# Cross attention of a perceiver layer: dividing the products instead of the probabilities, with the inverses sent round through DRAM

## The chip, the cores and the metric

The kernel runs on one core of a Trainium2 chip. The core has engines that work side by side, each through its own queue of instructions in a fixed order: TensorE (PE in the profile; loads of its stationary operand are PEld), VectorE (DVE), ScalarE (ACT) and GpSimd (POOL), and SyncE (SP), which here only issues transfers. They meet through semaphores. The metric is the device time of one execution in microseconds. Three runs of the kernel before took 698.24, 698.39 and 699.4 us; the median is 698.39.

## The reference, cut to what matters

The input is `x` (32 batches of 64 latents, 128 wide), a context (32 batches of 1601 tokens, 128 wide) and a mask of the context's tokens. The layer is a cross attention, a self attention and a feed-forward part, each added to `x`; only the first concerns the change.

```python
xn = layernorm(x, ln_x_g, ln_x_b)              # here x is the context
ln = layernorm(latents, ln_l_g, ln_l_b)        # latents are the normalised x
q = ln @ Wq
kv = jnp.concatenate((xn, ln), axis=1) @ Wkv
k, v = jnp.split(kv, 2, axis=-1)
q, k, v = (heads(q) * scale, heads(k), heads(v))   # 16 heads of 64
sim = jnp.einsum('bhid,bhjd->bhij', q, k)
sim = jnp.where(mask_full[:, None, None, :], sim, max_neg)
attn = jax.nn.softmax(sim.astype(jnp.float32), axis=-1).astype(sim.dtype)
out = jnp.einsum('bhij,bhjd->bhid', attn, v)
out = out.transpose(0, 2, 1, 3).reshape(b, m, INNER) @ Wout
return layernorm(out, ln_o_g, ln_o_b)
...
x = x + _L0_xattn_ref(ctx_1024, _layernorm(x, axis=-1), mask_BxS2_bk0, ...)
x = x + _L0_attn_ref(_layernorm(x, axis=-1), ...)
x = x + _L0_ffn_ref(_layernorm(x, axis=-1), ...)
```

The mask is true for the tokens that are used, and in this input those are at most the last 400 of a batch, beside the 64 latents, which are always keys too. The kernel sorts the batches by need and gives each 64 to 448 rows of context, so its rows are short.

## The kernel before, in words

**Weights.** For each head the kernel multiplies query and key weights into one 128 x 128 matrix (`a_sb`), and value and output weights into another (`b_sb`). So keys and values are never built: logits are products of the queries `qT` with the normalised tokens `xT`, the probabilities are multiplied with the same tokens (`xn`), and `b_sb` turns the result into the output.

**Tiles.** The 32 batches are sorted by the number of tokens that they need and paired, one long (u = 0) with one short (u = 1), into 16 tiles `t`. `CAPS` gives the rows: 512 logits beside 128 in the first eight tiles, 512 beside 256 in one, 384 beside 256 in six, 384 beside 384 in the last. At run time the kernel chooses among three arms by the mask; this input takes the narrow one, in which a step does both batches.

**Steps.** A step is one pair of heads `c` (0 to 7) of one tile, 128 steps in all. On its 128 partitions lie 2 heads x 64 latents. `logits` (line 522) does, for each u: a matmul into a PSUM bank `bank_s` (line 537, there are two such banks), one VectorE instruction that adds the mask's addends, writes the sums to `s` and finds the extreme `low` (line 540), and one ScalarE instruction that takes the exponential in place and sums the rows into `den` (line 545). Then VectorE takes the reciprocal of `den` (line 551), and multiplies each `s` with it (line 554).

`turned` transposes the probabilities on TensorE, two steps later (lines 573 and 583, copied to `pT` by ScalarE at 576 and 584). `attend` (line 590) runs after odd steps, three steps later for u = 0 and four for u = 1: it multiplies `xn` with the probabilities of two pairs of heads, for 256 columns in a bank `bank_m` (line 601), and VectorE copies the bank to `oT` (line 606). In `oT` the 128 partitions are the width of a token, not heads and latents. `project` (line 632) multiplies with `b_sb`, and adds and normalises.

**What runs in between.** Work of other tiles is laid beside the steps by `at(step, ...)`: the queries of the next tile (line 513), the normalising of its context (`prepare`: VectorE, GpSimd for a power at line 438, ScalarE at line 471), its transposes, the loads of the tile after it, and the self attention of the tile before (lines 654 to 778). The softmax of the self attention uses a bank `bank_s` too, which VectorE empties at line 719; line 774 adds the self attention's output to `x`.

**Order.** The lists made by `at` give the order of the program's text. The framework's scheduler then lays the instructions of each engine into one fixed order when the program is built, so that instructions can stand a little earlier or later than in the text. Within an engine's queue nothing overtakes. SP's queue holds the transfers of the loop: the context of tile t + 2 (lines 414 and 417, in up to two pieces), its mask (line 424) and `x` (line 403). The first piece waits until TensorE is done with the buffer's former tokens (there are three buffers).

**After the loop** come the feed-forward part and the stores (lines 885 to 988), with nothing of the cross attention.

Of the kernel before, what the change touches and what calls it, by code (L numbers as in the profile page):

```python
# [8 lines left out]
FP = mybir.dt.float32  # L9
# [3 lines left out]
ALU = mybir.AluOpType  # L13
# [3 lines left out]
P = 128  # L17
D = 128
B = 32
SL = 64  # L20
# [16 lines left out]
def perceiver_layer(  # L37
# [8 lines left out]
    nc = tc.nc  # L46
# [5 lines left out]
    early = ExitStack()  # L52
    look = early.enter_context(tc.tile_pool(name="look", bufs=1, side="right"))
    small = ctx.enter_context(tc.tile_pool(name="small", bufs=4))
    ps_s = ctx.enter_context(tc.tile_pool(name="ps_s", bufs=2, space=PSUM))
    ps_t = ctx.enter_context(tc.tile_pool(name="ps_t", bufs=3, space=PSUM))
    ps_m = ctx.enter_context(tc.tile_pool(name="ps_m", bufs=3, space=PSUM))
# [4 lines left out]
    def bank_m():  # L62
        return ps_m.tile([P, 512], FP, tag="m", name="bank_m")

    def bank_s():
        return ps_s.tile([P, 512], FP, tag="s", name="bank_s")


    def piece(eng, shape, src, name, pool=prep, dtype=FP):
        r = pool.tile(shape, dtype, name=name, tag=name)  # L70
        eng.dma_start(out=r, in_=src)
        return r
# [45 lines left out]
    for cap in sorted(set(CAPS), reverse=True):  # L118
# [7 lines left out]
        out=back, in0=mk, in1=back, scale=1.0, scalar=0.0,  # L126
# [10 lines left out]
    for r in range(0, B, 8):  # L137
        nc.vector.max(out=rank[:, r : r + 8], in_=left)
        if r + 8 < B:
            nc.vector.match_replace(  # L140
                out=left, in_to_replace=rank[:, r : r + 8], in_values=left, imm_value=-1.0
# [152 lines left out]
    for k, clip in enumerate((clip_x, clip_down)):  # L294
        c = piece(nc.scalar, [P, 1], clip.partition_broadcast(P), f"clip{k}", const)
# [55 lines left out]
    def attention(actx, name, caps):  # L351
# [6 lines left out]
        two = actx.enter_context(tc.tile_pool(name=f"two{name}", bufs=2))  # L358
        narrow = max(caps) <= SW
# [4 lines left out]
        def shape(t, u):  # L364

            nt, rest = divmod(cap(t, u) - SL, P)
            return nt, rest, [P] * (1 + nt) + [rest] * (rest > 0), SL + cap(t, u)
# [29 lines left out]
            for i in range(2):  # L397
                nc.gpsimd.memset(vxs[i], 0.0)

        masks, lns, lnTs, xTs, qTs, oTs, probs, pTs = {}, {}, {}, {}, {}, {}, {}, {}  # L400

        def load_x(t, u):
            nc.sync.dma_start(
# [117 lines left out]

        def logits(t, c, us):

            den = small.tile([P, len(us)], FP, tag=f"den{name}", name="den")
            for i, u in enumerate(us):
                sk = shape(t, u)[3]
                w = qTs[t][:, u, 2 * c : 2 * c + 2, :].rearrange("p h i -> p (h i)")
                s = two.tile(
                    [P, k_max[u]], FP, tag=f"s{u}" if narrow else "s", name=f"s{t}_{u}_{c}",
                    bufs=4 if narrow else 2,  # L530
                )[:, :sk]

                pieces = [(k, min(k + 512, sk)) for k in range(0, sk, 512)]
                low = small.tile([P, len(pieces)], FP, tag=f"low{name}{u}", name="low")
                for j, (k, e) in enumerate(pieces):
                    ps = bank_s()
                    nc.tensor.matmul(  # L537
                        ps[:, : e - k], lhsT=w, rhs=xTs[t, u][:, k:e], start=True, stop=True
                    )
                    nc.vector.tensor_tensor_reduce(  # L540
                        out=s[:, k:e], in0=ps[:, : e - k], in1=addends[u][t % NA][:, k:e],
                        scale=-1.0, scalar=3e38 if j == 0 else low[:, j - 1 : j],
                        op0=ALU.add, op1=ALU.min, accum_out=low[:, j : j + 1],
                    )
                nc.scalar.activation(  # L545
                    s, s, AF.Exp, bias=low[:, len(pieces) - 1 :], scale=-1.0,
                    accum_out=den[:, i : i + 1],
                )
                probs[t, u, c] = s
            rden = small.tile([P, len(us)], FP, tag=f"rden{name}", name="rden")  # L550
            nc.vector.reciprocal(rden, den)  # L551
            for i, u in enumerate(us):
                s = probs[t, u, c]
                nc.vector.tensor_scalar_mul(s, s, rden[:, i : i + 1])  # L554

        def turned(t, c, u):

# [32 lines left out]
        def attend(t, c, u):  # L590

            if t not in oTs:
                oTs[t] = two.tile(
                    [P, H, 2, SL], FP, tag="oT", name=f"oT{t}", bufs=2 if narrow else 1
                )
            pT = pTs.pop((t, u, c))
            po = bank_m()
            xn = xns[u][t % NX]
            tiles = shape(t, u)[2]
            for n, k in enumerate(tiles):  # L600
                nc.tensor.matmul(  # L601
                    po[:, : 2 * P], lhsT=xn[:k, n, :],
                    rhs=pT[:k, n].rearrange("p o c -> p (o c)"),
                    start=(n == 0), stop=(n == len(tiles) - 1),
                )
            nc.vector.tensor_copy(  # L606
                oTs[t][:, 2 * c : 2 * c + 4, u, :],
                po[:, : 2 * P].rearrange("p (h i) -> p h i", i=SL),
            )

        def moments(src, twice=False):
# [182 lines left out]
        for i, (t, c, us) in enumerate(steps):  # L794
            for u in us:
                at(i + 2, turned, t, c, u)
                if c % 2:
                    at(i + 3 + (u if narrow else 0), attend, t, c - 1, u)
# [71 lines left out]
        for i in range(max(later) + 1):  # L870
            if i < len(steps):
                logits(*steps[i])
            for f, args in later.get(i, ()):
                f(*args)
# [5 lines left out]
    for k in tc.Switch(which, 3):  # L880
        with ExitStack() as actx:
            attention(actx, "abc"[k], (CAPS, [SW] * B, [S2] * B)[k])


    with ExitStack() as fctx:
# [41 lines left out]
        for i in range(NB):  # L927
# [8 lines left out]
            for c, w in enumerate(widths):  # L936
# [6 lines left out]
                h = hT[i][:w, c, :]  # L943
# [89 lines left out]
```

## Time and profile before

| | |
|---|---|
| median of three runs | 698.39 us |
| the profiled execution: its own time | 700.29 us |
| the profiled execution: span, first to last instruction | 698.6 us |
| granted clock of TensorE, mean | 0.962 |
| busy: TensorE, VectorE, ScalarE, GpSimd | 622.9, 522.9, 409.2, 129.1 us |
| line 554, multiplying the probabilities | 256 instructions, 89.1 us |
| line 551, reciprocals | 128 instructions, 20.5 us |
| line 606, emptying the bank of `attend` | 128 instructions, 53.3 us |
| transfers of the execution | 12.00 MB, 17 GB/s over the span |

The page of the profile tells of one execution. Busy time is the sum of the instructions' durations on an engine; neighbours can overlap at their ends, and the end of a matmul is modelled, so a distance between two starts tells more than a duration. A line of a group reads: line of the kernel, engine, operation, output and inputs with shapes, count | busy us, mean ns of one | idle us of the engine just ahead of these instructions, and what ended it. A wait reads: who, for whom, us in total, how often, the longest. A line of a timeline reads: start, duration, instruction, count, and in brackets the idle time before it.

### The profile page before, as it was taken

Reading aid. Unit: us, or ns where it says so; the run is one execution under the profiler, and the core shown is the slowest. Engines: PE = TensorE matmul, PEld = TensorE weight load, DVE = VectorE, ACT = ScalarE, POOL = GpSimd, SP = SyncE. Lnnn points to the kernel's source line nnn. Section 1 sums busy time; section 2 is a strip of 40 time slices with the busy share of each in tenths; the row PEclk is TensorE's granted clock in tenths of the full one; section 3 lists DMA queues with packets and bytes.
Section 4 is the critical chain, followed back from the end, with each engine's and each line's share of the span. In section 5 each row is a group of like instructions: output and inputs, shape, how many; then the busy total and the mean of one; then the engine's idle time right before and its main releaser. Section 6 shows DMA issues by size and latency. Waiting matters only on the chain.

```text
span 698.6 us, 14235 instructions
## 1 busy us (share of the span) xinstructions
PE 622.9 (89%) x4798; PEld 498.9 (71%) x4798; DVE 522.9 (75%) x1991; ACT 409.2 (59%) x1095; POOL 129.1 (18%) x268
## 2 busy tenths in 40 slices
PE   3488999989898989899999999999999999955975
PEld 2357787868686868686878888888888886843335
DVE  7475778696868687878878888888888778644673
ACT  1456667666675657576666666666666566513341
POOL 2428220212121212111120212121212000010002
PEclk9789999999999999999999999999999999975987
DMA  6210101010101000000001010001010000000002
GB/s 170 64 39 1 24 2 23 1 24 1 24 1 24 2 26 4 15 10 15 10 2 25 1 24 1 24 1 24 1 28 1 1 1 1 1 1 4 0 0 62
DMA packets 20498, 12.00 MB, mean 17 GB/s; under 512 B 7632, under 2 KB 19952, under 8 KB 20416
## 3 DMA queue, kind: packets, MB, share of 16 engines
q1 hardware_dynamic: 15904, 8.70, 5.2%
q10 hardware_dynamic: 4352, 2.14, 1.2%
q8 instruction: 40, 0.66, 0.4%
q14 instruction: 42, 0.34, 0.2%
q0 software_dynamic: 160, 0.16, 0.1%
HBM read 9.94 MB, written 1.05 MB: 16 GB/s over the span
## 4 chain that ended last, share of the span: by engine, by line
PE 49%; DVE 26%; ACT 8%; issue 6%; POOL 5%; SPq 1%; DMA 1%; POOLq 0%; DVEq 0%; ACTq 0%
PE bank_m L601 11%; PE bank_s L537 10%; PE bank_m L632 6%; ACT s L545 5%; PE bank_m L513 5%; DVE s L540 5%; DVE s L554 5%; POOL rstd L438 5%; PE bank_t L583 4%; PE bank_s L939 3%; PE bank_t L203 3%; PE bank_m L966 2%; DVE oT L606 2%; PE bank_t L573 2%; PE bank_m L757 1%
## 5 line engine op out<-in xcount | busy, mean ns | idle before, releaser
L545 ACT ACTIVATE s<-s,low 128x512 f32<-128x512 f32 (+3 forms) x256 | 143.8, 563 | 102.7 <-DVE low L540 86.8
L537 PE MATMUL bank_s<-xT,qT 128*128 128x512 f32 (+3 forms) x512 | 171.0, 451 | 23.2 <-DVE low L540 12.1
L601 PE MATMUL bank_m<-pT,xn 128*128 128x256 f32 x656 | 166.5, 381 | 0.9 <-ACT pT L584 0.7
L537 PEld LDWEIGHTS bank_s<-xT,qT 128*128 128x128 f32 x512 | 89.2, 195 | 81.6 <-DVE p L719 20.9
L438 POOL TENSOR_TENSOR rstd<-rstd,mhalf 128x1 f32<-128x1 f32 (+2 forms) x96 | 61.2, 639 | 419.5 <-DVE rstd L434 402.6
L601 PEld LDWEIGHTS bank_m<-pT,xn 128*128 128x128 f32 x656 | 118.5, 191 | 17.7 <-ACT pT L584 2.5
L540 DVE CUSTOM_DVE_ANT_0 s<-bank_s,ad 128x512 f32<-128x512 f32 (+3 forms) x256 | 121.3, 487 | 10.0 <-PE bank_s L537 9.2
L584 ACT COPY pT<-bank_t 128x512 f32<-128x512 f32 (+1 forms) x136 | 70.4, 522 | 53.4 <-PE bank_t L583 53.2
L554 DVE TENSOR_SCALAR s<-s,rden 128x512 f32<-128x512 f32 (+3 forms) x256 | 89.1, 389 | 2.1
L583 PE MATMUL bank_t<-ident,s 128*128 128x128 f32 x480 | 75.8, 274 | 0.0
L583 PEld LDWEIGHTS bank_t<-ident,s 128*128 128x128 f32 x480 | 60.9, 141 | 12.5
L513 PE MATMUL bank_m<-lnT,a_sb 128*128 128x128 f32 x512 | 68.6, 279 | 0.4 <-ACT lnT L204 0.4
L513 PEld LDWEIGHTS bank_m<-lnT,a_sb 128*128 128x128 f32 x512 | 63.4, 196 | 0.7 <-ACT lnT L204 0.7
L632 PE MATMUL bank_m<-b_sb,oT 128*128 128x128 f32 x512 | 63.3, 276 | 0.5 <-DVE oT L606 0.5
L632 PEld LDWEIGHTS bank_m<-b_sb,oT 128*128 128x128 f32 x512 | 60.1, 192 | 1.7 <-DVE oT L606 1.2
L606 DVE COPY oT<-bank_m 128x256 f32<-128x256 f32 x128 | 53.3, 416 | 10.6 <-PE bank_m L601 10.4
L471 ACT ACTIVATE xn<-xn,shift,rstd 128x128 f32<-128x128 f32 x82 | 36.6, 489 | 29.4 <-DVE shift L467 29.4
L545 ACT ACTIVATION_READ_ACCUMULATOR s<-s,low 128x1 f32 x256 | 48.4, 189 | 0.0
L517 ACT COPY qT<-bank_m 128x512 f32<-128x512 f32 x64 | 37.3, 583 | 14.3 <-PE bank_m L513 13.8
L551 DVE RECIPROCAL rden<-den 128x2 f32<-128x2 f32 x128 | 20.5, 160 | 32.6 <-ACT s L545 31.6
L573 PE MATMUL bank_t<-ident,s 128*128 128x128 f32 x176 | 29.0, 273 | 0.0
L576 ACT COPY pT<-bank_t 128x256 f32<-128x256 f32 (+1 forms) x60 | 27.9, 465 | 0.0
(175 smaller groups left out, 864.4 us busy)
## 6 DMA issues: line engine op xcount, KB each, us to landing
xn<-in_ctx_dram SPq DMA_DIRECT2D x9, 192.0 KB, 2.4
x<-in_x_dram SPq DMA_DIRECT2D x32, 32.0 KB, 2.2
xn<-in_ctx_dram SPq DMA_DIRECT2D x32, 32.0 KB, 1.9
xn<-in_ctx_dram SPq DMA_DIRECT2D x8, 128.0 KB, 2.0
out_dram<-y SPq DMA_DIRECT2D x18, 32.0 KB, 1.8
wq_sb<-in_L_xattn_Wq_dram SPq DMA_DIRECT2D x1, 512.0 KB, 5.0
wk_sb<-in_L_xattn_Wkv_dram SPq DMA_DIRECT2D x1, 512.0 KB, 7.0
wv_sb<-in_L_xattn_Wkv_dram ACTq DMA_DIRECT2D x1, 512.0 KB, 6.2
```

Source lines behind the costliest of these rows:

```text
L438: nc.gpsimd.tensor_tensor(rstd, rstd, mhalf[:, :n], ALU.pow)
L513: nc.tensor.matmul(pm[:, j * P : (j + 1) * P], lhsT=a_sb[:, h4 + j, :], rhs=lnTs[t], start=True, stop=True,)
L537: nc.tensor.matmul(ps[:, : e - k], lhsT=w, rhs=xTs[t, u][:, k:e], start=True, stop=True)
L540: nc.vector.tensor_tensor_reduce(out=s[:, k:e], in0=ps[:, : e - k], in1=addends[u][t % NA][:, k:e], scale=-1.0, scalar=3e38 if j == 0 else ...
L545: nc.scalar.activation(s, s, AF.Exp, bias=low[:, len(pieces) - 1 :], scale=-1.0, accum_out=den[:, i : i + 1],)
L554: nc.vector.tensor_scalar_mul(s, s, rden[:, i : i + 1])
L573: nc.tensor.transpose(bt[:, n, o, :], s[:, n * P : (n + 1) * P], ident)
L583: nc.tensor.transpose(bt[:, j - n, :], s[:, j * P : (j + 1) * P], ident)
L584: nc.scalar.copy(pT[:, n:e, odd, :], bt[:, : e - n, :])
L601: nc.tensor.matmul(po[:, : 2 * P], lhsT=xn[:k, n, :], rhs=pT[:k, n].rearrange("p o c -> p (o c)"), start=(n == 0), stop=(n == len(tiles) - 1),
L606: nc.vector.tensor_copy(oTs[t][:, 2 * c : 2 * c + 4, u, :], po[:, : 2 * P].rearrange("p (h i) -> p h i", i=SL),)
L632: nc.tensor.matmul(pm[:, :D], lhsT=oT[:, h].rearrange("p u i -> p (u i)"), rhs=b_sb[:, h, :], start=(h == 0), stop=(h == H - 1),)
```

## The change

The probabilities stay as the exponential left them. The sums of an even and an odd step go into one tile `den` of four columns (for two batches). After the odd step VectorE takes one reciprocal of it in place. SP stores the four columns to DRAM (`line`, 128 partitions x 16 bytes), and reads the 512 numbers back to all 128 partitions (`rden`, 2 KB on each, three buffers). `attend` no longer copies its bank: VectorE multiplies it with the numbers of its own two pairs of heads and its own batch. These stand in `rden` four elements apart, since a partition of `den` holds four sums side by side.

```diff
     small = ctx.enter_context(tc.tile_pool(name="small", bufs=4))
+    dram = ctx.enter_context(tc.tile_pool(name="dram", bufs=4, space=bass.MemoryType.DRAM))
...
-            den = small.tile([P, len(us)], FP, tag=f"den{name}", name="den")
+            odd, n_us = c % 2, len(us)
+            if not odd:
+                sums[t, us[0]] = small.tile([P, 2 * n_us], FP, tag=f"den{name}", name="den")
+            den = sums[t, us[0]]
...
                 nc.scalar.activation(
                     s, s, AF.Exp, bias=low[:, len(pieces) - 1 :], scale=-1.0,
-                    accum_out=den[:, i : i + 1],
+                    accum_out=den[:, odd * n_us + i : odd * n_us + i + 1],
                 )
                 probs[t, u, c] = s
-            rden = small.tile([P, len(us)], FP, tag=f"rden{name}", name="rden")
-            nc.vector.reciprocal(rden, den)
-            for i, u in enumerate(us):
-                s = probs[t, u, c]
-                nc.vector.tensor_scalar_mul(s, s, rden[:, i : i + 1])
+            if odd:
+                nc.vector.reciprocal(den, den)
+                line = dram.tile([P, 2 * n_us], FP, tag=f"line{name}", name="line")
+                nc.sync.dma_start(out=line, in_=den)
+                rden = two.tile(
+                    [P, 2 * n_us * P], FP, tag="rden", name=f"rden{t}_{us[0]}_{c}",
+                    bufs=3 if narrow else 2,
+                )
+                nc.sync.dma_start(
+                    out=rden, in_=line.rearrange("p j -> (p j)").partition_broadcast(P)
+                )
+
+                view = rden.rearrange("d (h i o u) -> d u o h i", h=2, o=2, u=n_us)
+                for i, u in enumerate(us):
+                    sums[t, u, c - 1] = view[:, i]
...
-            nc.vector.tensor_copy(
-                oTs[t][:, 2 * c : 2 * c + 4, u, :],
-                po[:, : 2 * P].rearrange("p (h i) -> p h i", i=SL),
-            )
+            nc.vector.tensor_tensor(
+                oTs[t][:, 2 * c : 2 * c + 4, u, :].rearrange("p (o h) i -> p o h i", o=2),
+                po[:, : 2 * P].rearrange("p (o h i) -> p o h i", o=2, h=2),
+                sums.pop((t, u, c)), ALU.mult,
+            )
```

## The prediction

> **What bounds the kernel now.** I read the engine table first, then the stretches of 40 us, the waits of TensorE, one tile's timeline, and last the groups and transfers.
>
> ```profile
> PE 622.9 (89%) x4798; PEld 498.9 (71%) x4798; DVE 522.9 (75%) x1991; ACT 409.2 (59%) x1095; POOL 129.1 (18%) x268
> ...
> 200.00:240.00 40.00, 37.95 (x305) 30.57 (x304) 31.75 (x127) 24.93 (x69) 6.78 (x14) 1.00 0.05 12
> ```
>
> The second line is one stretch of the loop: TensorE is busy 37.95 of 40 us at full clock, VectorE 31.75. The chain of waits gives PE 49% and DVE 26%, so it must be asked how much of TensorE's time is idle at all. Over 80 to 600 us, which holds nearly the whole loop, its waits are:
>
> ```profile
> PE bank_s L537 <- DVE p L719: 10.6, 12, 1.1
> PE bank_s L537 <- DVE low L540: 6.9, 8, 1.7
> PE bank_t L658 <- DVE rden L551: 0.7, 1, 0.7
> PE bank_m L601 <- ACT pT L584: 0.7, 2, 0.4
> ```
>
> Columns: total us, times, longest. Both large ones are logits matmuls without a free `bank_s`, because VectorE is late with emptying it. In one tile:
>
> ```profile
> 212.41 0.67 DVE L554 TENSOR_SCALAR s<-s,rden 128x512 f32<-128x512 f32 x2
> 213.00 0.28 DVE L774 TENSOR_TENSOR x<-bank_m,x 128x128 f32<-128x128 f32 x1
> ...
> 215.23 0.49 PE L583 MATMUL bank_t<-ident,s 128*128 128x128 f32 x3
> 216.71 1.35 PE L537 MATMUL bank_s<-xT,qT 128*128 128x512 f32 x4 [0.99 <-DVE low L540]
> ...
> 222.69 0.49 PE L537 MATMUL bank_s<-xT,qT 128*128 128x128 f32 x2 [1.05 <-DVE p L719]
> ```
>
> Matmul ends are modelled, so I count idle by starts. Three transposes in a row elsewhere advance by 0.33, so TensorE was free at 215.56 and idled 1.15, not 0.99; likewise 1.22, not 1.05. About 0.17 goes on top of each wait: 10.6 + 6.9 + 20 x 0.17 = 20.9 us of real idle. Adding all matmul groups of this tile by starts gives 33.2 us of work in a period of 36.1 (the L537 waits recur at 144.52, 180.61, 216.71, 252.81). Later tiles repeat every 34.6 (405.08, 439.68). So TensorE is the bound, and VectorE costs at most some 21 us here. Outside the loop the change finds nothing: the waits at 42.84 and 61.75 us hang on GpSimd's work on the weights and the norms, and after 617 us no multiplied probability is left.
>
> ```profile
> L606 DVE COPY oT<-bank_m 128x256 f32<-128x256 f32 x128 | 53.3, 416 | 10.6 <-PE bank_m L601 10.4
> L554 DVE TENSOR_SCALAR s<-s,rden 128x512 f32<-128x512 f32 (+3 forms) x256 | 89.1, 389 | 2.1
> L551 DVE RECIPROCAL rden<-den 128x2 f32<-128x2 f32 x128 | 20.5, 160 | 32.6 <-ACT s L545 31.6
> L719 DVE TENSOR_TENSOR p<-bank_m,bias 128x256 f32<-128x256 f32 x32 | 13.3, 415 | 0.0
> xn<-in_ctx_dram SPq DMA_DIRECT2D x9, 192.0 KB, 2.4
> out_dram<-y SPq DMA_DIRECT2D x18, 32.0 KB, 1.8
> mask<-in_mask_BxS_bk_dram SPq DMA_DIRECT2D x9, 56.0 KB, 3.0
> mask<-in_mask_BxS_bk_dram SPq DMA_DIRECT2D x8, 8.0 KB, 2.6
> SPq L414 <- PE bank_m L601: 386.5, 25, 39.3
> ```
>
> Groups, then DMA issues (KB, us to landing), then the longest wait of SP's queue.
>
> **What the Trainium skill says.** "VectorE: DVE Perf Modes", § The perf-mode tier table: a float32 `tensor_scalar` in SBUF runs at twice the rate, `tensor_tensor` and float32 work from PSUM at one element a cycle. The trace agrees: L554 takes 489 ns for 512 and 286 for 128 (0.53 ns an element), L540 from PSUM 678 and 280 (1.04 ns), and a multiply in place of L606 should cost what L719 does, 415 against 416 ns. "SBUF — State Buffer", § Door 1 (note on cachelines): lines of 16 bytes, float32 strides free up to 4 elements, a penalty for an access that leaves its line. The new operand is read at a stride of exactly 4, and no row here shows that. "DMA: Bandwidth & Descriptors", § Anatomy of one DMA: some 2 us fixed, most of it the receipt of the write; 1.8 to 2.4 above agree. "SBUF — State Buffer", § Who interferes with whom: DMA doesn't contend with compute engines, so I charge the new traffic to its own latency only.
>
> **The change, part by part.** The input takes the narrow arm: 16 tiles of 8 steps, two batches a step.
>
> *Removed.* 256 multiplications L554 (89.1 us busy). By starts a pair costs about 0.60 us (208.58 to 209.18), so 128 x 0.60 = 77 us, 4.8 a tile. 128 reciprocals become 64 of four columns; they advance by about 0.08 to 0.2 us, so 0.3 to 0.8 a tile goes. With them goes VectorE's wait for ScalarE's exponentials (31.6 us), in half of the steps altogether. In the other half the built order puts the reciprocal of an odd step later, mostly behind work that is due anyway.
>
> *Changed.* 128 evacuations L606 become multiplications from PSUM. Free stride: +0. Half rate: 256 elements at 1.04 ns again, +0.27 each, 34 us in all, 2.1 a tile. A gain is excluded, since PSUM already sets the rate. The skill's text leans to free; I take 0.42.
>
> *Added.* 64 stores of 2 KB (16 bytes a partition) and 64 broadcasts of 256 KB to SP's queue: 128 issues of about 0.45 us, 58 us of a queue that otherwise mostly waits, and 16.8 MB more traffic. The store I take as 2.3 us (1.8 to 3). The broadcast lies between 2.4 (the rate of `xn`) and 4.7 (the masks' 0.4 us for 48 KB more, carried to 256 KB: 2.6 + 2.1); I take 3.
>
> *Does it arrive?* The reciprocals of odd steps are followed by the first evacuation that needs them 8 to 11 us later. The tightest is step 1: today L551 at 219.22, its evacuation at 228.94. In the built order the store follows the first context load on SP, which waits for TensorE (the 39.3 us wait above), and ahead of the broadcast stand the second load, the mask, a register load and the load of `x`. Today that series takes 3.3 us (79.75 to 83.09), longer than the store's landing. From the reciprocal: 3.2 + 3 = 6.2 us (5.6 to 7.9), against some 8.4 left once VectorE is earlier. It arrives, so hidden, at cost 0. What stands behind it on SP are only loads for two tiles ahead.
>
> *The first stall.* The order of TensorE is the same in both programs but for trifles, so I walk one tile with its starts fixed. VectorE reaches L774 once TensorE's L773 is done, at 212.3 instead of 213.0; without the multiplications nothing lies between. The rest up to the end of L540 (2.96 us from 213.0 to its start, 0.6 for itself) is unchanged but for 0.1, a wait for GpSimd included: `bank_s` is free at about 215.85 instead of 216.65. Idle falls from 1.15 to 0.3.
>
> *The second stall.* From there two pairs (1.2 us) and a reciprocal are gone, but two waits for GpSimd's power (0.6 each) come to lie bare, since nothing fills them now. I find L719 at about 220.4 instead of 222.24, with TensorE asking at 220.66 after a shift of 0.8: idle 1.22 becomes 0.1 to 0.2. A half-rate evacuation delays this by 0.15 to 0.6.
>
> *Sum.* First stall 8 x (0.86 + 0.17 - 0.3) = 5.9; second 12 x (0.88 + 0.17 - 0.15) = 10.8; single ones about 0.5. Together 17 us. The profiled execution took 700.29 with a span of 698.6, 1.9 above the median of 698.39; taken off each: 681.6 of span, 681.4 of time. I say 682.
>
> **Rivals.**
> 1. *The stride halves the evacuation.* For: the skill's own wording on lines; against: its figure of 4 elements as free. VectorE still falls by 3 us a tile, and only a part is in front of the stalls: 2 to 5 us of the gain goes, 685.5 (684 to 691).
> 2. *TensorE's idle comes back elsewhere.* For: the built order puts the fifth step's L540 behind the affine of the next keys, thus behind four L471 of ScalarE, and bares GpSimd's waits; by my walk the banks are still free 0.6 to 1.8 us ahead of need. If half the gain goes: 693 (690 to 697).
> 3. *The broadcast is late, and the kernel slower.* Then the evacuation stands at the head of VectorE's queue, and everything behind it, the emptying of `bank_s` first, stops TensorE. The place is step 1. 17 us over 15 tiles are 1.1 a tile, so it decides from 9.5 us after the reciprocal, a broadcast of about 6.3 us. At 8 us it is 2.8 late: 15 x 2.8 - 17 = +25, 723. For: 128 rows read one place in memory, and a mask of 8 KB needs 2.6. Against: 6.3 is twice any steady transfer here.
> 4. *No difference*: the gain and a small lateness cancel, 698.
>
> **How the numbers follow.** Forecast 0.58 (676 to 687), rival 1 0.20, rival 2 0.10, rival 3 0.09, no difference 0.03. A change under 0.2% (1.4 us) is about what a measurement of this kernel can't tell from none. Faster 0.88, same 0.03, slower 0.09. No less than 698.4 - 20.9 - 1.4 = 676 is possible from the waits counted; the range begins just below, at 675.5, and ends at 691, with rival 1 inside and rivals 2 and 3 left out in the main.
>
> **What would show it.** Right: the multiplication rows gone, VectorE's busy time near 424 us (522.9 - 89.1 - 64 x 0.16; 458 at half rate), the evacuation at about 0.42 us with no wait for a transfer, L537's waits near 4 us, periods of about 34.2 and 33.6. Wrong: an evacuation waiting for `rden`; SP's broadcasts landing after more than 6 us; TensorE waiting for ScalarE; a granted clock under 1.00 in the loop, which would make busier TensorE slower.

## The result: slower, and the profile after

The changed kernel takes 709.29 us (median of four runs, 707.68 to 710.59) against 698.89 for the kernel before beside it (698.24 to 700.0): a ratio of 1.0146, 95% interval 1.0119 to 1.0172. Its profiled execution took 710.59 us with a span of 708.8.

From the page: the engine table, and the chain of work that ended last.

```profile
PE 632.0 (89%) x4798; PEld 504.8 (71%) x4798; DVE 473.0 (67%) x1671; ACT 411.1 (58%) x1095; POOL 126.9 (18%) x268
...
PE 72%; DVE 13%; DMA 4%; issue 2%; POOL 2%; SPq 1%; ACT 1%; DVEq 0%; POOLq 0%; ACTq 0%
```

VectorE has 50 us less to do, as the change meant it to, and its share of the chain has fallen from 26% to 13%. The share of DMA in the chain has grown from 1% to 4%, and it is `xn`, the context. The evacuation and the statistics of the context in the changed kernel, and the statistics in the kernel before (busy us, mean ns | idle ahead of them):

```profile
L623 DVE TENSOR_TENSOR oT<-bank_m,rden 128x256 f32<-128x256 f32 x128 | 80.1, 626 | 26.6 <-PE bank_m L618 25.9
...
L464 DVE BATCH_NORM_STATS2 st<-xn 128x6 f32<-128x128 f32 x82 | 21.3, 287 | 21.7 <-DMA xn<-in_ctx_dram 21.7
...
L463 DVE BATCH_NORM_STATS2 st<-xn 128x6 f32<-128x128 f32 x82 | 21.3, 277 | 3.0 <-DMA xn<-in_ctx_dram 3.0
```

The evacuation (L623) never waits for the broadcast, so the inverses are in time. But `L464`, the statistics of a context tile, now waits 21.7 us for its load; in the kernel before the same line (L463) waited 3.0. The transfers of the changed kernel (KB, median us from issue to landing), and the waits of TensorE between 80 and 600 us:

```profile
rden<-line SPq DMA_DIRECT2D x64, 256.0 KB, 3.8
xn<-in_ctx_dram SPq DMA_DIRECT2D x9, 192.0 KB, 3.5
...
line<-den SPq DMA_DIRECT2D x64, 2.0 KB, 1.4
```

```profile
PE bank_s L544 <- DVE p L737: 17.2, 12, 2.6
PE bank_s L544 <- DVE low L547: 4.1, 6, 0.7
```

The second stall, for the emptying of `bank_s` by the self-softmax (L737), has not gone: it grew from 10.6 to 17.2 us, the longest from 1.1 to 2.6. The first fell from 6.9 to 4.1. Two stretches of the loop, the second of 4 us (columns as before: busy us of TensorE, its weight loads, VectorE, ScalarE, GpSimd, then the granted clock, the transfers' share and GB/s):

```profile
200.00:240.00 40.00, 39.02 (x368) 31.33 (x367) 29.55 (x108) 26.56 (x75) 7.24 (x16) 1.00 0.19 38
...
404.00:408.00 4.00, 4.00 (x18) 3.33 (x19) 4.00 (x12) 0.74 (x2) 0.00 (x0) 0.62 0.29 93
```

At 200 to 240 us TensorE is busier than before, as forecast (39.02 against 37.95), at full clock. At 404 it has just stopped for 2.3 us, and its clock is at half for most of the stretch. What stopped it, from the timeline of the changed kernel:

```profile
399.05 0.16 DVE L558 RECIPROCAL den<-den 128x4 f32<-128x4 f32 x1
...
399.24 0.32 SPq L560 DMA_DIRECT2D line<-den  x1
...
400.14 0.52 SPq L415 DMA_DIRECT2D xn<-in_ctx_dram  x1
...
400.67 0.81 PE L544 MATMUL bank_s<-xT,qT 128*128 128x384 f32 x2
...
402.86 0.29 DVE L464 BATCH_NORM_STATS2 st<-xn 128x6 f32<-128x128 f32 x1 [2.58 <-DMA xn<-in_ctx_dram]
...
403.29 0.39 DVE L737 TENSOR_TENSOR p<-bank_s,bias 128x256 f32<-128x256 f32 x1
...
403.74 1.22 PE L544 MATMUL bank_s<-xT,qT 128*128 128x256 f32 x2 [2.26 <-DVE p L737]
```

and the same place in the kernel before:

```profile
401.54 0.47 SPq L414 DMA_DIRECT2D xn<-in_ctx_dram  x1
...
403.41 0.81 PE L537 MATMUL bank_s<-xT,qT 128*128 128x384 f32 x2
...
404.22 0.28 DVE L463 BATCH_NORM_STATS2 st<-xn 128x6 f32<-128x128 f32 x1
...
404.63 0.39 DVE L719 TENSOR_TENSOR p<-bank_s,bias 128x256 f32<-128x256 f32 x1
```

Take the logits matmul of 384 columns as the mark. The load is issued 1.87 us ahead of it before (401.54 to 403.41), 0.53 after, 1.34 us later. With the lead of before it would have been due at 398.80; SP stood in the store's wait for the reciprocal until 399.24 (0.44), and the load follows the store by 0.90. VectorE reaches the statistics 0.81 behind the mark before, and 0.39 ahead of it after (402.86 - 2.58 = 400.28): 1.20 earlier. The load took 2.1 us before and lay ready 0.6 ahead of need; it took 2.7 after. 1.34 + 1.20 + 0.6 (landing) - 0.6 (reserve) = 2.54, against the 2.58 shown. Behind the statistics stands the emptying of `bank_s`, and for that TensorE waits.

### The profile page after: what moved, and what is told of

It reads as the page before. It is cut to its first block, busy times and chain, and to the rows that moved or that the text cites. A ratio compares the mean times of both kernels' runs of the same rounds, so it can differ in the third digit from the quotient of the medians.

```text
span 708.8 us, 14264 instructions
## 1 busy us (share of the span) xinstructions
PE 632.0 (89%) x4798; PEld 504.8 (71%) x4798; DVE 473.0 (67%) x1671; ACT 411.1 (58%) x1095; POOL 126.9 (18%) x268
## 4 chain that ended last, share of the span: by engine, by line
PE 72%; DVE 13%; DMA 4%; issue 2%; POOL 2%; SPq 1%; ACT 1%; DVEq 0%; POOLq 0%; ACTq 0%
PE bank_m L618 18%; PE bank_s L544 17%; PE bank_m L650 8%; PE bank_m L514 8%; PE bank_t L600 6%; PE bank_t L204 4%; DMA xn<-in_ctx_dram 4%; PE bank_s L957 3%; PE bank_m L775 2%; PE bank_t L590 2%; DVE s L547 2%; PE bank_m L984 2%; POOL rstd L439 2%; DVE oT L623 1%; DVE st L632 1%
## 5 line engine op out<-in xcount | busy, mean ns | idle before, releaser
L544 PE MATMUL bank_s<-xT,qT 128*128 128x512 f32 (+3 forms) x512 | 171.4, 452 | 25.0 <-DVE p L737 17.2
L618 PE MATMUL bank_m<-pT,xn 128*128 128x256 f32 x656 | 170.6, 388 | 0.6 <-ACT pT L601 0.4
L618 PEld LDWEIGHTS bank_m<-pT,xn 128*128 128x128 f32 x656 | 120.7, 194 | 18.5 <-ACT pT L601 2.0
L623 DVE TENSOR_TENSOR oT<-bank_m,rden 128x256 f32<-128x256 f32 x128 | 80.1, 626 | 26.6 <-PE bank_m L618 25.9
L600 PE MATMUL bank_t<-ident,s 128*128 128x128 f32 x480 | 77.1, 277 | 0.0
L514 PE MATMUL bank_m<-lnT,a_sb 128*128 128x128 f32 x512 | 70.1, 283 | 0.4 <-ACT lnT L205 0.4
L514 PEld LDWEIGHTS bank_m<-lnT,a_sb 128*128 128x128 f32 x512 | 65.2, 200 | 0.7 <-ACT lnT L205 0.7
L464 DVE BATCH_NORM_STATS2 st<-xn 128x6 f32<-128x128 f32 x82 | 21.3, 287 | 21.7 <-DMA xn<-in_ctx_dram 21.7
L590 PE MATMUL bank_t<-ident,s 128*128 128x128 f32 x176 | 30.3, 282 | 0.0
L957 PE MATMUL bank_s<-xqT,guT 128*128 128x512 f32 (+1 forms) x48 | 25.2, 651 | 0.3
```

The costliest lines, as they stand in the source:

```text
L514: nc.tensor.matmul(pm[:, j * P : (j + 1) * P], lhsT=a_sb[:, h4 + j, :], rhs=lnTs[t], start=True, stop=True,)
L544: nc.tensor.matmul(ps[:, : e - k], lhsT=w, rhs=xTs[t, u][:, k:e], start=True, stop=True)
L590: nc.tensor.transpose(bt[:, n, o, :], s[:, n * P : (n + 1) * P], ident)
L600: nc.tensor.transpose(bt[:, j - n, :], s[:, j * P : (j + 1) * P], ident)
L618: nc.tensor.matmul(po[:, : 2 * P], lhsT=xn[:k, n, :], rhs=pT[:k, n].rearrange("p o c -> p (o c)"), start=(n == 0), stop=(n == len(tiles) - 1),
L623: nc.vector.tensor_tensor(oTs[t][:, 2 * c : 2 * c + 4, u, :].rearrange("p (o h) i -> p o h i", o=2), po[:, : 2 * P].rearrange("p (o h i) - ...
```

## The experiments

**Theory A**: the late load is what makes the kernel slower, by way of statistics that stand in front of `bank_s`. **Theory B**: the evacuation at half rate. **Theory C**: the traffic of the broadcasts, or a clock that falls by itself. The letters in the expectations are those of each run; where one differs, the text says so. In the runs with a tile of ones and in the changed kernel with a fourth buffer, the small tile `blk` of the preparations also has one buffer instead of four; it is used once.

### The two halves of the change, each alone

The division is left out, and the evacuation multiplies by ones:

```diff
-                line = dram.tile(...); nc.sync.dma_start(out=line, in_=den)
-                rden = two.tile(...);  nc.sync.dma_start(out=rden, in_=line...)
+                rden = same[:, : 2 * n_us * P]        # a tile of ones
```

> The changed kernel without the stores and the broadcasts: the evacuation multiplies by a tile of ones at the same stride of 4, so the division by the sums is left out. The removal is alone, with the half-rate evacuation, and nothing new on SP. Theory A: the loads are where they were in the kernel before, but VectorE comes earlier to the statistics and waits for them by about 1.2 us a tile (the load lands 0.6 us ahead of need in the kernel before, VectorE is about 1.2 to 1.8 earlier), so the second stall stays at about 0.9 and only the first goes: no half-clock windows, 686 to 694. Theory B: as slow as with the transfers, 704 to 711. If the removal alone gave all that was forecast: 680 to 684.

Measured: 690.56 us, ratio 0.9868 (0.9842 to 0.9894).

TensorE's waits at `bank_s` between 80 and 600 us (L731 is the self-softmax):

```profile
PE bank_s L546 <- DVE p L731: 4.1, 11, 0.8
PE bank_s L546 <- DVE low L549: 4.1, 6, 0.7
```

The clock is full throughout the loop. So the removal gains 9.5 us of the 700.07 beside it, half-rate evacuation included, and the transfers cost 19 us on top of it. The statistics do wait for the load, by 0.5 to 0.6 us in most of the later tiles, less than A's 1.2, since the load is back at 1.87 us ahead of the mark (393.66 to 395.53).

The kernel before with the stores and broadcasts only:

```diff
             nc.vector.reciprocal(rden, den)
+            if c % 2:
+                nc.sync.dma_start(out=line, in_=rden)
+                nc.sync.dma_start(out=wide, in_=line.rearrange("p j -> (p j)").partition_broadcast(P))
```

> The kernel before with stores of the inverses (1 KB, of odd steps only) and broadcasts of 128 KB added on SP's queue, whose product nobody reads; the multiplications and the plain evacuation stay. Order of TensorE and VectorE as before but for trifles. Theory A: the context load comes about 1.3 us later with a slack of 0.6, so the statistics wait some 0.7 us a tile and the kernel is slower, 700 to 710, with VectorE's wait at the statistics over 8 us in all (3.0 before). Theory B: 697 to 700, nothing to see, since the evacuation is not touched.

Measured: 713.56 us, ratio 1.0192 (1.0164 to 1.022): more than A's range. VectorE waits 10.7 us at the statistics between 80 and 600 us. The first emptying of `bank_s` is at 120.51 (114.00 before), after waits of 1.88, 1.70 and 1.55; the distance stays at 6.3 to 6.5 until 301.24 and is 17.6 at 422.22. After that nothing more is lost: there the first piece of the load is ahead of the store on SP (419.13 and 419.77), and ahead of the emptying VectorE has only that piece's statistics. Of the two tiles between, the first has the same order on SP, but the statistics of the second piece, behind the store (334.68, 335.44), stand ahead of the emptying too and wait 3.23. The second of them:

```profile
378.00 0.32 SPq L555 DMA_DIRECT2D line<-rden  x1
...
378.89 0.47 SPq L415 DMA_DIRECT2D xn<-in_ctx_dram  x1
...
383.09 0.29 DVE L464 BATCH_NORM_STATS2 st<-xn 128x6 f32<-128x128 f32 x1 [1.55 <-DMA xn<-in_ctx_dram]
...
384.42 0.49 DVE L464 BATCH_NORM_STATS2 st<-xn 128x6 f32<-128x128 f32 x2 [0.82 <-DMA xn<-in_ctx_dram]
...
385.28 1.22 PE L538 MATMUL bank_s<-xT,qT 128*128 128x256 f32 x2 [3.54 <-DVE p L730]
```

Here the pieces (the second was issued at 379.63) also land late, 4.2 and 4.8 us after their issue, where the kernel before needs 1.9 to 2.4. So the transfers do two things to a load: they hold up its issue, and they lengthen its landing. B has no part in this run.

The same is seen inside the changed kernel. When each tile's `bank_s` was emptied first (L719, L737, L731), in us:

| tile's emptying | before | changed | without transfers |
|---|---|---|---|
| first | 114.00 | 109.58 | 111.37 |
| fifth | 258.34 | 250.07 | 252.25 |
| eighth | 370.01 | 365.09 | 361.62 |
| thirteenth | 543.29 | 553.45 | 533.44 |

From the second to the fifth tile SP has the store between the two pieces of the load (246.88, 247.45 and 248.20 in the fifth). Only the first piece's statistics stand ahead of the emptying, VectorE doesn't wait for them, and a tile takes 35.1 us, 1.0 less than before. In the sixth SP's order is the same, but the second piece's statistics stand ahead of the emptying too (286.94). From the seventh to the twelfth the store is ahead of both pieces. All seven of these wait, 1.09 to 2.93 us each, and the kernel loses 22 us to the one without transfers (from 2.2 ahead to 20.0 behind).

### A fourth context buffer

```diff
-        NX, NA = (3, 2) if narrow else (1, 1)
+        NX, NA = (4, 2) if narrow else (1, 1)
```

> The changed kernel with a fourth context buffer, so that a context tile may be loaded a whole tile earlier; nothing else differs but the order that follows from it. Theory A (late loads: the context load stands behind the store of the inverses on SP's queue, the statistics on VectorE wait for it, bank_s is emptied late, TensorE stops and its clock halves): VectorE's wait at L464 falls from 21.7 us to under 3, the half-clock windows in the loop go, TensorE's wait at L544 for p falls from 17.2 to under 6, time 678 to 690. Theory B (the evacuation at 626 ns, read at a stride of 4, makes VectorE late by itself): a buffer changes nothing, 704 to 711. Theory C (TensorE's clock falls in the loop for a reason of its own): windows at half clock stay, 700 or more.

> The kernel before with the fourth context buffer alone. Theory A: its context load is just in time (lands 0.6 us before the statistics), so hardly anything is won: 694 to 699, TensorE's waits at bank_s within 3 us of before. If the load bounded the second stall of the kernel before already, these waits fall from 17.5 to under 10 and the time to 685 to 692.

Measured: 713.09 us on the changed kernel, ratio 1.0204 (1.0168 to 1.0241), and 699.16 on the kernel before, 0.9996 (0.9979 to 1.0013). The second is 0.2 above A's range, with TensorE's waits at `bank_s` at 16.9 us in all against 17.5, as A had it. The first is a miss; by its time and its waits alone it would sooner fit B or C.

```profile
PE bank_s L544 <- DVE p L737: 18.8, 11, 3.0
...
DVE st L464 <- DMA xn<-in_ctx_dram: 20.1, 9, 3.0
```

Nothing was cured. In the built order the statistics ahead of the emptying are those of the buffer loaded just then, with three buffers and with four (1, 2, 3, 0 in turn). The fourth buffer moved load and statistics together one tile further ahead, and left no time between them; that the scheduler places statistics by when it takes their load to have landed is inferred from this order. So the run doesn't test A: the load is as late for its reader as it was. Depth isn't reserve when the reader is moved too.

### The statistics behind the self-softmax

```diff
+                emptied[0] = nc.vector.tensor_reduce(stat[:, hs], p[:, hs], AX.X, ALU.max)
...
+            with tc.issue_after(emptied[0].ins) if emptied[0] else ExitStack():
                 for n in range(n_all):
                     nc.vector.bn_stats(out=st[:, n, :], in_=xn[:, n, :])
```

> The changed kernel with one rule of order for VectorE: the statistics of a context tile are issued behind the last self-softmax issued so far instead of right ahead of it. SP's order, and so the place of the context loads behind the stores of the inverses, is that of the changed kernel. Theory A (the late load harms only because the statistics stand ahead of the emptying of bank_s): TensorE's wait at L544 for p falls from 17.2 us to under 6, no half-clock window in the loop, 685 to 694, like the kernel without transfers at 690.6. Theory B (transfers slow the kernel wherever VectorE takes up their data, by their traffic or their landing): the wait moves to another place, over 700.

Measured: 685.16 us, ratio 0.9787 (0.9766 to 0.9808). The one wait of TensorE at `bank_s` (80 to 600 us), and its timeline at the same place as above:

```profile
PE bank_s L546 <- DVE low L549: 4.3, 7, 0.7
```

```profile
389.68 0.32 SPq L562 DMA_DIRECT2D line<-den  x1
...
390.58 0.52 SPq L416 DMA_DIRECT2D xn<-in_ctx_dram  x1
...
391.07 1.24 PE L546 MATMUL bank_s<-xT,qT 128*128 128x384 f32 x4
...
391.13 0.42 DVE L737 TENSOR_TENSOR p<-bank_s,bias 128x256 f32<-128x256 f32 x1 [0.45 <-PE bank_m L725]
```

The load is as late as before, 0.9 us behind the store, with every transfer in place (192 KB even land in 4.0 us). But the emptying doesn't stand behind it, and TensorE goes through its four matmuls without a stop. The second stall is gone and the clock is full in the loop. This settles A against B, whose half rate is still here, and against C, which this run's expectation calls B. It is the version that beats both kernels.

The rule alone, in the kernel before, and the rule without transfers (by ones again, so undivided):

> The kernel before with the same rule of order for VectorE as in the run with the statistics behind the self-softmax; multiplications, reciprocals and plain evacuation stay, no transfers are added. If the rule alone won the 15 us of that run: 682 to 688. Theory A: in the kernel before the load was just in time, so the rule only takes the statistics' own 0.4 to 0.7 us a tile from in front of bank_s: 690 to 697, and the change with the rule stays 5 us and more ahead of it.

> The kernel without transfers (690.6; the evacuation multiplies by ones at a stride of 4, so the division by the sums is left out) with the statistics behind the self-softmax. If the transfers cost nothing once the statistics do not wait in front of bank_s: 683 to 686, the same as with them (685.2). If their traffic still costs something: 678 to 682.

Measured: 693.37 us, ratio 0.9907 (0.9872 to 0.9942), and 682.43 us, ratio 0.9764 (0.9734 to 0.9794). So the rule is worth 0.9% by itself (TensorE's wait for L719 falls from 10.6 to 3.4 us, that for `low` grows from 6.9 to 9.3), and under the rule the change is worth 0.9787 / 0.9907, or 1.2%. Transfers and all, it stands 0.2% from the run without them. These two intervals overlap, and 682.43 lies between the ranges of its two expectations: whether the traffic costs anything there is open.

### The store on another queue

```diff
-                nc.sync.dma_start(out=line, in_=den)
+                nc.gpsimd.dma_start(out=line, in_=den)
```

> The changed kernel with the 64 stores of the inverses on GpSimd's queue; the broadcasts stay on SP, and TensorE's and ScalarE's orders are the same. The context load no longer stands behind a wait for VectorE's reciprocal. Theory A: the load is issued about 1.3 us earlier in the tiles after 300 us, VectorE's wait at the statistics falls from 2.5 to 2.9 us a tile to 0.6 to 1.3, half-clock windows go, 688 to 697 (GpSimd's powers behind a waiting store may cost up to 3 of it). Theory C (not the order but the traffic of the broadcasts makes the load land late): waits stay at 2 us and more, 703 to 710.

Measured: 696.56 us, ratio 0.9944 (0.9932 to 0.9956).

```profile
400.48 0.47 SPq L415 DMA_DIRECT2D xn<-in_ctx_dram  x1
...
401.24 0.60 POOL L560 DMA_DIRECT2D line<-den  x1 [0.16 <-issue]
...
402.56 0.30 DVE L464 BATCH_NORM_STATS2 st<-xn 128x6 f32<-128x128 f32 x1 [0.58 <-DMA xn<-in_ctx_dram]
```

With the broadcasts unchanged the load is back at 1.87 us ahead of the mark (402.35) and lands in 2.1 us again, the wait in the last five tiles of this kind is 0.54 to 0.67, and no half-clock stretch is left in the loop. So it was the store on SP there, not the traffic of the broadcasts. One tile still waits 2.63 us (329.80), for a load that took 4.5 us to land; no run tells why. In the profiled executions this run loses 2.3 us to the one without transfers up to the first emptying (113.63), 2.5 more up to the sixth (35.7 a tile against 35.1 to 35.4) and 2.0 in the tile of that wait, of 8.0 at the thirteenth. GpSimd waits 128.7 us in the store for the reciprocal, with the norms' powers behind it; that this costs the rest is argued, not shown.

### The evacuation's rate

Unit stride, without the transfers (`same` read as `d (u o h i)`, undivided) and with them, each inverse then paired with another row:

> The kernel without transfers (690.6), with the tile of ones read at unit stride instead of a stride of 4; the same orders on every engine, and the division by the sums is left out as there. Evacuations fall from about 626 to about 416 ns, 27 us of VectorE in all. If the half rate costs what its share of the stalls is: 685 to 689; if it is hidden: 690 to 691; if the rest of the forecast gain is there: 682 to 684.

> The changed kernel with the inverses read at unit stride, so that each product is multiplied by the inverse of another row (the pairing is left wrong; the transfers and all orders are the same). Theory A: a VectorE that is earlier only waits longer for the same load: the evacuation takes 416 ns, the time stays at 704 to 710. Theory B (the half-rate evacuation is what makes the kernel slower): 690 to 699.

Measured: 688.0 us, ratio 0.9825 (0.9789 to 0.9861), and 712.08 us, ratio 1.0174 (1.0109 to 1.0239). The evacuation takes 419 ns in both; with the transfers:

```profile
L623 DVE TENSOR_TENSOR oT<-bank_m,rden 128x256 f32<-128x256 f32 x128 | 53.7, 419 | 28.6 <-PE bank_m L618 28.4
```

The half rate costs some 2.6 us where nothing else is in the way (690.56 to 688.0; the intervals just overlap, so this is not clear of noise), and nothing that can be seen in the changed kernel. There VectorE's wait at the statistics between 80 and 600 us grew from 17.8 to 23.3 us, and the time lies 2 us above A's range. B falls.

A store that turns the rows itself, so that the broadcast could be read at unit stride, added to the run with the statistics behind the self-softmax (685.16). The view read by the evacuation has batch and step exchanged, so some products get the inverse of another row here too; the rest is as in that run:

```diff
+                line = dram.tile([2 * n_us, P], FP, ...)
+                nc.sync.dma_start(out=line.rearrange("j p -> p j"), in_=den)
```

> The changed kernel with the statistics behind the self-softmax (685.2) and the inverses stored in the order in which the products lie: the store writes 512 pieces of 4 bytes instead of 128 of 16, and the evacuation reads the broadcast at unit stride. Evacuation 419 ns instead of 626. If the store lands within about 1 us more than its 1.4: 682 to 685 (the unit stride was worth 2.6 us without transfers). If it lands 4 us later and more: evacuations wait for the broadcast, 690 to 720.

Measured: 949.41 us, ratio 1.3539 (1.3465 to 1.3612), far above both ranges.

```profile
xn<-in_ctx_dram SPq DMA_DIRECT2D x9, 192.0 KB, 10.2
...
line<-den SPq DMA_DIRECT2D x64, 2.0 KB, 10.9
```

The store of the same 2 KB lands in 10.9 us instead of 1.5, and evacuations wait 258.1 us for broadcasts. The packets went from 38926 to 63503, which is 64 x 384 and 1 more (512 pieces instead of 128), as the Trainium skill has it ("DMA: Bandwidth & Descriptors", § Rules for kernel authors: a last dimension that isn't contiguous becomes one descriptor an element). This is what the prediction's third rival looks like when it happens.

## Why the prediction was wrong

**The step that failed** is the last sentence of *Does it arrive?*: "What stands behind it on SP are only loads for two tiles ahead", priced at 0. The loads are for two tiles ahead, but their first reader isn't two tiles later. It stands on VectorE right ahead of the emptying of `bank_s`, 2.7 us behind the load's issue (401.54 to 404.22), with 0.6 us in reserve. I costed the waiting store by who waits for the store, and not by who waits for what is queued behind it. Nor did the order read at step 1, the store behind the first piece of the load, hold for all tiles: from the seventh to the twelfth the store is ahead of it. The price was 19 us between the medians, 20.0 between the profiled executions. TensorE's two waits at `bank_s` are 13.1 us longer than without transfers (17.2 + 4.1 against 8.2), and the stretches at half clock take 10.2 us of full clock (summed over the 4 us stretches from 284 to 524 us), a small part of it in the waits themselves. Against these 23 us stand the 2.2 by which the changed kernel was ahead at the fifth tile. The last of the prediction's warnings, a granted clock under 1.00 in the loop, came true, though through idle time and not through busier work.

**The second stall** failed for a related reason: the walk moved L719 forward with VectorE's work and left the load in front of it out. Without transfers 4.1 us of the 10.6 stay, where I had left some 0.15 a tile.

**Removed**: the multiplications and half of the reciprocals went as counted. The groups' busy time falls by 89.1 + 9.2 and rises by 26.8 for the evacuation, 71.5 less in all; the engine table shows 49.9 less. It counts overlapping ends once, and is not the plain sum of durations that the text ahead of the prediction calls it (VectorE's groups before add to some 627 us, the table has 522.9). So taking the groups' time off the table's could not come out: 473.0 stands against the 458 forecast for half rate.

**Changed**: mis-sized. The upper of the two values was right: 626 against 416 ns, +0.21 for each where I had +0.27, 26.8 us in all. The first rival's mechanism is so; it is worth about 2.6 us without transfers, inside its 2 to 5 but not clear of noise.

**Added**: the store takes 1.4 us (I took 2.3), the broadcast 3.8 (I took 3, of 2.4 to 4.7). That the new traffic doesn't slow the compute engines agrees: the exponentials take 563 ns before and after. The reckoning that the inverses arrive was right: no evacuation waits for them. What I did not charge is the landing of the loads beside them: 192 KB in 3.5 us instead of 2.4, 128 KB in 2.5 instead of 2.0.

**The sum**: 17 us of gain were forecast for the removal. With the transfers out and the statistics behind the emptying it is 1 - 0.9764 = 2.4%, or 16.5 us. That agrees in part by chance: the tiles take 34.8 and 34.0 us there, not 34.2 and 33.6, and 5.4 us are won ahead of the first emptying (108.62 against 114.00), where I had counted hardly anything: my stalls are those after 80 us.

**The rivals**: the second (idle comes back elsewhere) was nearest to the truth, but put it behind ScalarE and GpSimd, and stopped at half the gain. The third had the right shape, VectorE's queue held up by a transfer in front of `bank_s`, with the wrong transfer.

## What to carry to other kernels

Before putting a transfer that waits on a compute engine into a queue shared with loads, find the first reader of every load behind it, in the built order, and what stands behind that reader. A load "for two tiles ahead" has no reserve if the built order has its reader just behind the landing; here a further buffer didn't help, and a rule that keeps the reader behind the urgent work did. An engine made faster comes to its next wait earlier, so look for the waits that lie just ahead of zero today.

## What the runs showed of the hardware

- Stops of TensorE as short as 2.3 us went with a halved clock. In the changed kernel all half clock between 80 and 600 us lies at five stops of 2.26 to 2.62 us; at the one before 403.74 it lasted from 403.6 to 407.0, 3.4 us. A stop of 2.31 ahead of 441.90 cost none, nor did one of 3.01 with the fourth buffer (293.67). In the kernel before, with no stop above 1.75 us there, the clock stays full. The Trainium skill ("TensorE: Matmul & The Clock Gate", § What's actually happening) tells of a free-running window of 3413 ns; the length agrees, and that equal stops differ fits a window that runs free, though the stops here are shorter than the idle window of about 3.4 us that its table asks for.
- A float32 operand in SBUF at a stride of four elements makes `tensor_tensor` half as long again here: 626 ns for 256 elements against 419 at unit stride, with the other operand from PSUM in both. The skill's note on cachelines ("SBUF — State Buffer", § Door 1) calls strides up to four free; the measurement decides.
- A 2 KB store in 512 pieces of 4 bytes takes 10.9 us to land, in 128 pieces of 16 bytes 1.5, and the loads in the same queue land later beside it (192 KB in 10.2 us against 4.0).
- Behind a 2 KB store on SP the next load was issued 0.90 us after it (399.24 and 400.14 in the changed kernel, 389.68 and 390.58 with the statistics behind).
